# A layer norm inside a scheduled Mamba block: the sum of squares by VectorE or GpSimd and four narrow matmuls, in place of twelve column-group matmuls

## The chip, the cores and the metric

The kernel runs on one core of a Trainium2 chip, as one launch. The metric is the device time of that launch in microseconds (us), as the median of several runs. The profile is one execution of the same program, and its span is counted from the first to the last instruction that the profiler recorded. Engines are named as the profile names them: PE is TensorE's matmuls, PEld its weight loads, DVE is VectorE, ACT is ScalarE, POOL is GpSimd, and SP is SyncE, which issues nearly all DMAs.

## The reference

The input is x of shape (8, 384, 32, 32), taken as eight batches of 1024 tokens with 384 channels. Everything is float32.

```
x = x + mamba(ln_c(x))          # eight batches
t = t + ffn(ln_t(t))            # t = tokens of x; only batches 0 to 4 change

mamba:  t = layernorm(t) * ln_w + ln_b
        xm, z = split(t @ in_proj_w.T)         # 384 -> 2 x 768
        xc = silu(causal_conv3(xm) + conv_b)
        dt, Bm, Cm = split(xc @ x_proj_w.T)    # 24 + 16 + 16
        dt = softplus(dt @ dt_proj_w.T + dt_proj_b)
        h_t = exp(dt*A) * h_(t-1) + dt*xc*Bm ;  y = sum_n h*Cm + xc*D   # 16 states
        t = (y * silu(z)) @ out_proj_w.T
        t = gelu(t @ mlp_w1.T + b1) @ mlp_w2.T + b2
ffn:    two linear layers with sign-binarised weights, each output clipped and
        scaled by the largest absolute value of its batch, a gelu between them
```

Each norm takes a mean and a variance over the 384 channels of a token, subtracts the mean and multiplies by (variance + eps) to the power of -1/2. The reference's norm of x and the first norm of the Mamba block are joined into one in the kernel.

## The kernel before

**Tiles.** Channels lie on the 128 partitions and tokens along the free axis. A batch is cut into two halves of T = 512 tokens, so a normalised tile is [128, 3, 512]: KC = 3 chunks of 128 channels. G = 4, and TG = 128 tokens is a quarter of a half.

**Stages.** For each batch, `s1` does the norm, the input projections (`p_in`, `p_z`), the convolution, the low-rank projection (`p_dbc`, `p_all`, then `p_dt`), and writes its results to DRAM. `s2` does the scan: POOL multiplies, ACT takes the exponential, DVE runs the scan instruction (line 990), and PE adds over the states (`py`, line 929, 1536 matmuls in all, 192 to a batch). `s3` does the output projection and the MLP (`p_out`, `p_h`, `p_o`). `ffn` runs for batches 0 to 4 (`p_y1` and `p_y2`, which the profile shows as p_y).

**The norm.** `norm` (lines 590 to 666) is called 26 times: twice for each of the eight batches in `s1`, and twice for each of five batches in `ffn`. Its steps are, in order: `total` is the sum of the three chunks, by POOL with two adds (lines 628 and 629) or by DVE with one reduction (line 632); a matmul with a 128x128 block of ones gives -C times the mean on every partition (`p_mean`, line 640); DVE subtracts it (line 643); ACT squares the tile into `sq` (line 557). Then `columns` (line 599) sums the squares over the channels: three chunks by four token quarters, twelve matmuls with a [128, 32] block of ones, the quarters lying in four 32-column groups of the array. ACT or DVE scales the sums into SBUF (`var`, line 572 or 579). One matmul with every 32nd column of the identity (`p_turned`, line 654) turns them so that tokens lie on partitions, as [128, 4]. DVE adds eps (line 658), POOL takes the power (line 660), `spread` (line 617) brings the four columns back to a row on all partitions (`p_r`), and DVE multiplies (line 664).

**The order of the work.** Nothing runs in the order in which it is written down. Each step is handed to a planner (`Plan.add`) with an engine, a cost in us, the tiles that it reads and writes, and optionally another engine that may do it (`others`). `Plan.run` then plays the engines forward with those costs, takes the next step for the engine that is free first, and emits the instructions in that order. So a changed step can move any later instruction on any engine. Three more rules of the planner matter here:

- A tile comes from a ring with a fixed number of buffers: `mm` (PSUM) has three, `sq` two, `rstd` two, `root` two, and `dbc` one. A step waits until its ring has a free buffer. In the kernel before, `dbc` is used by the low-rank projection of `s1` alone: from `p_dbc` until `p_dt` has read it and the store `rows_d<-dbc` is done.
- PE pays 0.097 us (`MODE`) in the planner's books whenever it changes between column- or row-tiled matmuls (`tiled=True`) and full ones.
- Where PE would stand idle for over 0.7 us in those books (`IDLE`), the planner emits matmuls whose result nobody reads (`spare`, line 451, 128x256), until the gap is filled. These are real instructions of the program:

```
if e == "PE":
    while now - free[e] > IDLE and self.spare.ring.free[0:] and (...):
        ...
        self.fill()
        free[e] = clock.run(free[e], MM / 2)
```

Every float32 matmul shows up in the trace as two passes: two weight loads and two matmul records.

Of the kernel before, what the change touches and what calls it, by code (L numbers as in the profile page):

```python
# [28 lines left out]
ALU = mybir.AluOpType  # L29
AX = mybir.AxisListType  # L30
# [3 lines left out]
P = 128  # L34
B, C, L = 8, 384, 1024
KC = C // P
# [8 lines left out]
T = 512  # L45
HALVES = [slice(0, T), slice(T, L)]
SQ = 4
DQ = P // SQ
# [4 lines left out]
G = P // DQ  # L53
TG = T // G
# [37 lines left out]
def c_act(n):  # L92
    return 0.2 + n * 0.00084


def c_dve(n):
    return 0.17 + n * 0.00102
# [90 lines left out]
class Plan:  # L188
# [12 lines left out]
    def add(self, engine, cost, emit, r=(), w=(), claim=(), table=None, size=0, others=None,  # L201
            land=1.6, rate=350e3, lag=None, tiled=False):
        op = Op()
        op.engine, op.cost, op.emit, op.table = engine, cost, emit, table
        op.others, op.settle = others or {}, None
        op.size, op.land, op.prio = 0.03 + size / rate, land - 0.1, (*self.prio, len(self.ops))
        op.next, op.ready, op.tiles, op.tiled = [], 0.0, [], tiled
        op.lag = LAG.get(engine, 0.0) if lag is None else lag
        op.slack = SLACK if self.prio[0] < 0 else 0.0
        deps = set()  # L210

        def parts_of(t):
            t, part = t if isinstance(t, tuple) else (t, None)
            if t not in op.tiles:
                op.tiles.append(t)
                if t.ring is not None:
                    t.left += 1
            if part is None:
                if None not in t.parts:
                    t.parts[None] = [None, []]  # L220
                return list(t.parts.values())
            if part not in t.parts:
                whole = t.parts.get(None)
                t.parts[part] = [whole[0], list(whole[1])] if whole else [None, []]
            return [t.parts[part]]

        for t in claim:
            t.left += 1
            op.tiles.append(t)
        for t in r:  # L230
            for p in parts_of(t):
                if p[0] is not None:
                    deps.add(p[0])
                p[1].append(op)
        for t in w:
            for p in parts_of(t):
                if p[0] is not None:
                    deps.add(p[0])
                deps.update(p[1])
                p[0], p[1] = op, []  # L240
        deps.discard(op)
        op.wants = len(deps)
        for d in deps:
            d.next.append(op)
        self.ops.append(op)
        return op
# [144 lines left out]
class Layer:  # L391
# [198 lines left out]
    def norm(self, t, eps, scale):  # L590

        nc, add = self.nc, self.plan.add
        def columns(src, name):
            p = self.piece("mm", [P, TG], name)

            def emit():
                for k in range(KC):
                    for g in range(G):
                        nc.tensor.matmul(
                            p.real[g * DQ : (g + 1) * DQ, :], self.ones[:, :DQ],  # L600
                            src.real[:, k, g * TG : (g + 1) * TG],
                            start=(k == 0), stop=(k == KC - 1),
                        )

            add("PE", 0.79, emit, r=[src], w=[p], tiled=True)
            return p

        def spread(src, name, turned=False):
            p = self.piece("mm", [P, T], name)

            def emit():
                for g in range(G):
                    if turned:
                        by, of = src.real[:, g : g + 1], self.ident
                    else:
                        by, of = self.ident[:, g * DQ : g * DQ + 1], src.real
                    nc.tensor.matmul(
                        p.real[:, g * TG : (g + 1) * TG], by.to_broadcast([P, P]), of,
                        start=True, stop=True,
                    )  # L620

            add("PE", 0.89, emit, r=[src], w=[p])
            return p

        total = self.piece("sq", [P, T], "total")

        def in_two():
            nc.gpsimd.tensor_add(total.real, t.real[:, 0, :], t.real[:, 1, :])
            nc.gpsimd.tensor_add(total.real, total.real, t.real[:, 2, :])

        def at_once():
            nc.vector.tensor_reduce(
                total.real, t.real.rearrange("p k l -> p l k"), AX.X, ALU.add
            )

        add("POOL", 2.5, in_two, r=[t], w=[total], others={
            "DVE": (c_dve(KC * T) + 0.02, at_once)
        })
        p_mean = self.piece("mm", [P, T], "p_mean")
        add("PE", MM, lambda: nc.tensor.matmul(  # L640
            p_mean.real, self.ones, total.real, start=True, stop=True
        ), r=[total], w=[p_mean])
        add("DVE", c_dve(KC * T) + 0.05, lambda: nc.vector.scalar_tensor_tensor(
            t.real, p_mean.real.unsqueeze(1).to_broadcast([P, KC, T]), -1.0 / C, t.real,
            ALU.mult, ALU.add,
        ), r=[p_mean], w=[t])

        sq = self.piece("sq", [P, KC, T], "sq")
        self.act(lambda: sq.real, lambda: t.real, AF.Square, c_act(KC * T), r=[t], w=[sq])
        p_var = columns(sq, "p_var")  # L650
        var = self.piece("rstd", [P, TG], "var")
        self.affine(lambda: var.real, lambda: p_var.real, [p_var], [var], scale=scale, n=TG)
        p_turned = self.piece("mm", [P, G], "p_turned")
        add("PE", 0.14, lambda: nc.tensor.matmul(
            p_turned.real, var.real, self.ident[:, ::DQ], start=True, stop=True
        ), r=[var], w=[p_turned])
        rstd = self.piece("root", [P, G], "rstd")
        add("DVE", 0.15, lambda: nc.vector.tensor_scalar_add(rstd.real, p_turned.real, eps),
            r=[p_turned], w=[rstd])
        add("POOL", 1.0, lambda: nc.gpsimd.tensor_tensor(  # L660
            rstd.real, rstd.real, self.power.to_broadcast([P, G]), ALU.pow
        ), w=[rstd])
        p_r = spread(rstd, "p_r", True)
        add("DVE", c_dve(KC * T), lambda: nc.vector.tensor_mul(  # L664
            t.real, t.real, p_r.real.unsqueeze(1).to_broadcast([P, KC, T])
        ), r=[p_r], w=[t])
# [738 lines left out]
```

## Time and profile before

| | |
|---|---|
| runs | 3205.4, 3207.55, 3211.03 us; median 3207.55 |
| profiled execution | 3206.13 us, span 3204.3 us, so 1.8 us lie around the span |
| granted TensorE clock, mean | 0.987 |
| busy in the span | PE 3087.3, POOL 2803.7, DVE 2602.2, ACT 2021.0 us |
| DMA | 751.78 MB, 235 GB/s over the span |

A group of the profile is written as "line engine operation out<-in, shapes, count, then busy us and mean ns of one, then the idle time of the engine just before these instructions and what ended it". In the chain of waits each piece is what released the next one, followed back from the last instruction. A PE record lasts until the result is out, and records overlap, so the busy time of a group is the better price of a matmul than the mean of one record.

### The profile page before, as it was taken

To read this page: it belongs to the slowest core of one execution; us is meant where nothing else is said; L and a number is where in the kernel's file an instruction comes from. 1 tells how busy PE (TensorE), PEld (TensorE's weight loads), DVE (VectorE), ACT (ScalarE), POOL (GpSimd) and SP (SyncE) were. 2 spreads that over 40 slices of the span, in tenths; PEclk is the share of its full clock that TensorE was granted. 3 is DMA by queue.
4 is the path that set the end of the run, shared out by engine and by line. 5 is a ranking of instruction groups with operands and counts; after the bars stand their busy time and mean duration, and the time that the engine had idled before them with its cause. 6 is when DMAs were issued, how large, how long until landed. Compare 5 with 4: busy or idle time off the path is not lost.

```text
span 3204.3 us, 32487 instructions
## 1 busy us (share of the span) xinstructions
PE 3087.3 (96%) x10286; PEld 1265.2 (39%) x10286; DVE 2602.2 (81%) x2058; ACT 2021.0 (63%) x2397; POOL 2803.7 (87%) x1097
## 2 busy tenths in 40 slices
PE   9898999998999999999999999999999999999999
PEld 4333433343433443444344334343344443333333
DVE  4787887889978789787898888997788977887881
ACT  4878786767666565665675576457566565655662
POOL 2878988989989888999988999999989999998890
PEclk9899999999999999999999999999999999999999
DMA  7888878767777667766687686777768756756542
GB/s 236 293 290 303 272 230 305 267 213 250 241 287 249 202 204 248 261 229 221 207 296 239 212 301 213 253 229 278 239 223 268 235 184 216 232 179 191 162 153 72
DMA packets 348970, 751.78 MB, mean 235 GB/s; under 512 B 36480, under 2 KB 113792, under 8 KB 339584
## 3 DMA queue, kind: packets, MB, share of 16 engines
q1 hardware_dynamic: 348368, 749.61, 70.3%
q8 instruction: 83, 1.36, 0.2%
q14 instruction: 87, 0.71, 0.1%
q10 hardware_dynamic: 432, 0.09, 0.0%
HBM read 569.21 MB, written 180.36 MB: 234 GB/s over the span
## 4 chain that ended last, share of the span: by engine, by line
PE 62%; DVE 12%; DMA 9%; POOL 7%; ACT 6%; issue 3%; SPq 1%; DVEq 0%; POOLq 0%; ACTq 0%
PE p_y L541 15%; PE p_h L541 11%; PE p_o L541 10%; PE py L929 8%; PE p_out L541 6%; POOL u L965 5%; PE p_z L541 5%; PE p_in L541 5%; DVE u L990 4%; DVE da L990 3%; ACT da L557 2%; DMA dtx_r<-dtx_d 2%; ACT L557 2%; DMA dt_r<-dt_d 1%; PE spare L451 1%
## 5 line engine op out<-in xcount | busy, mean ns | idle before, releaser
L557 ACT ACTIVATE da<-dt_r,a_neg 128x1024 f32<-128x1024 f32 (+1 forms) x960 | 898.9, 944 | 596.0 <-DVE u L990 320.4
L965 POOL TENSOR_TENSOR u<-dtx_r,bc 128x2048 f32<-128x2048 f32 (+1 forms) x360 | 1185.5, 3309 | 87.6 <-PE py L929 49.1
L965 POOL TENSOR_TENSOR u<-u,bc 128x2048 f32<-128x2048 f32 (+1 forms) x274 | 900.0, 3291 | 140.9 <-DVE u L990 129.2
L990 DVE TENSOR_TENSOR_SCAN u<-da,u 128x1024 f32<-128x1024 f32 (+1 forms) x436 | 869.9, 2007 | 160.2 <-ACT da L557 80.6
L541 PE MATMUL p_h<-t,w_b 128*128 128x512 f32 x1152 | 515.7, 601 | 16.5 <-DMA w_b<-in_mlp_w 13.8
L541 PE MATMUL p_o<-g,w 128*128 128x512 f32 x1152 | 514.5, 600 | 6.4 <-DMA w<-in_mlp_w 4.7
L990 DVE TENSOR_TENSOR_SCAN da<-da,dtx_r 128x1024 f32<-128x1024 f32 (+1 forms) x192 | 382.0, 2015 | 64.0 <-POOL dtx_r L965 45.0
L965 POOL TENSOR_TENSOR dtx_r<-dtx_r,bc 128x2048 f32<-128x2048 f32 (+1 forms) x120 | 396.6, 3310 | 1.9
L541 PEld LDWEIGHTS p_h<-t,w_b 128*128 128x128 f32 x1152 | 215.0, 191 | 307.7 <-issue 264.0
L541 PEld LDWEIGHTS p_o<-g,w 128*128 128x128 f32 x1152 | 216.3, 191 | 298.0 <-issue 280.2
L541 PE MATMUL p_y<-tn,w_b 128*128 128x512 f32 x720 | 320.1, 600 | 7.7 <-DVE tn L664 3.4
L541 PE MATMUL p_y<-gf,w_n 128*128 128x512 f32 x720 | 321.9, 600 | 5.4 <-ACT dt L572 2.6
L929 PE MATMUL py<-u,fold 128*32 128x512 f32 x2304 | 306.7, 630 | 7.5 <-POOL u L965 7.5
L990 DVE TENSOR_TENSOR_SCAN da<-da,u 128x1024 f32<-128x1024 f32 (+1 forms) x140 | 281.8, 2038 | 34.0 <-ACT da L557 18.4
L557 ACT ACT_TABLE_LOAD x211 | 270.7, 1283 | 6.5 <-DMA dt_r<-dt_d 2.8
L541 PE MATMUL p_out<-yg,w 128*128 128x512 f32 x552 | 244.9, 596 | 3.4 <-ACT dt L572 1.8
L541 PE MATMUL p_in<-t,w_f 128*128 128x512 f32 x504 | 230.2, 605 | 15.5 <-ACT t L572 4.4
L541 PE MATMUL p_z<-t,w_f 128*128 128x512 f32 x504 | 232.4, 609 | 12.3 <-DMA w_f<-in_in_proj_w 7.7
L541 PEld LDWEIGHTS p_y<-tn,w_b 128*128 128x128 f32 x720 | 135.0, 191 | 189.5 <-issue 168.3
L541 PEld LDWEIGHTS p_y<-gf,w_n 128*128 128x128 f32 x720 | 134.6, 191 | 189.3 <-issue 170.9
L572 ACT ACTIVATE y<-p_y,v_vecs 128x512 f32<-128x512 f32 x145 | 98.8, 681 | 130.7 <-PE p_y L541 104.0
L572 ACT ACTIVATE g<-p_h,v_vecs 128x512 f32<-128x512 f32 x159 | 108.0, 679 | 114.1 <-PE p_h L541 113.6
(132 smaller groups left out, 3267.4 us busy)
## 6 DMA issues: line engine op xcount, KB each, us to landing
dtx_r<-dtx_d SPq DMA_DIRECT2D x72, 1024.0 KB, 6.0
dt_r<-dt_d SPq DMA_DIRECT2D x144, 512.0 KB, 5.1
w_b<-in_mlp_w SPq DMA_DIRECT2D x192, 192.0 KB, 3.4
w<-in_mlp_w SPq DMA_DIRECT2D x96, 384.0 KB, 3.3
w_f<-in_in_proj_w SPq DMA_DIRECT2D x168, 192.0 KB, 4.6
y_d<-y SPq DMA_DIRECT2D x120, 256.0 KB, 4.8
gf<-y_d SPq DMA_DIRECT2D x60, 512.0 KB, 6.7
xc_d<-xc SPq DMA_DIRECT2D x48, 512.0 KB, 6.5
```

The source lines that it names most:

```text
L451: self.plan.fill = lambda: self.nc.tensor.matmul(self.plan.spare.real[:, : 2 * P], self.ones, self.one.to_broadcast([P, 2 * P]), start=Tru ...
L541: self.nc.tensor.matmul(p.real, w.real[:, w0 + k, :], t.at(k0 + k), start=start and k == 0, stop=stop and k == n - 1,)
L557: lambda: self.nc.scalar.activation(out(), in_(), func, **{k: v() if callable(v) else v for k, v in kw.items()}),
L572: nc.scalar.activation(out(), in_(), AF.Identity, bias=bias, scale=scale)
L929: nc.tensor.matmul(py.real[g * DQ : (g + 1) * DQ, :], self.fold, hc, start=False, stop=(q == NQUAD - 1), skip_group_check=True,)
L965: nc.gpsimd.tensor_mul(u.real[:, x], t.real[:, x], row.real.unsqueeze(2).to_broadcast([P, n, 2]))
L990: da=da, in_u=in_u: nc.vector.tensor_tensor_scan(to(i), da.real[:, i, :], in_u(i), state.real[:, col : col + 1] if half else 0.0, ALU.mult ...
```

## The change

The twelve matmuls of `columns`, the scaled copy `var` and the matmul that turned it are taken out. The squares of the three chunks are added into a [128, 512] tile `squared`: by DVE with one reduction, or by POOL with two adds where the planner finds POOL free. Four matmuls then take a quarter of `squared` each as weights and a single column of ones as the moving operand, which sums over the channels and turns in one step. The scale moves into the instruction that adds eps. The tile `squared` comes from the ring `dbc`; `var` no longer takes a buffer of the ring `rstd`, and `p_var` none of the ring `mm`. The new matmuls are not marked as tiled, and the planner books them with 0.56 us, where it booked 0.79 for `columns` and 0.14 for the turn.

```diff
     def norm(self, t, eps, scale):
 
         nc, add = self.nc, self.plan.add
-        def columns(src, name):
-            p = self.piece("mm", [P, TG], name)
-
-            def emit():
-                for k in range(KC):
-                    for g in range(G):
-                        nc.tensor.matmul(
-                            p.real[g * DQ : (g + 1) * DQ, :], self.ones[:, :DQ],
-                            src.real[:, k, g * TG : (g + 1) * TG],
-                            start=(k == 0), stop=(k == KC - 1),
-                        )
-
-            add("PE", 0.79, emit, r=[src], w=[p], tiled=True)
-            return p
-
...
         sq = self.piece("sq", [P, KC, T], "sq")
         self.act(lambda: sq.real, lambda: t.real, AF.Square, c_act(KC * T), r=[t], w=[sq])
-        p_var = columns(sq, "p_var")
-        var = self.piece("rstd", [P, TG], "var")
-        self.affine(lambda: var.real, lambda: p_var.real, [p_var], [var], scale=scale, n=TG)
+        squared = self.piece("dbc", [P, T], "squared")
+
+        def two_sums():
+            nc.gpsimd.tensor_add(squared.real, sq.real[:, 0, :], sq.real[:, 1, :])
+            nc.gpsimd.tensor_add(squared.real, squared.real, sq.real[:, 2, :])
+
+        def one_sum():
+            nc.vector.tensor_reduce(
+                squared.real, sq.real.rearrange("p k l -> p l k"), AX.X, ALU.add
+            )
+
+        add("DVE", 1.83, one_sum, r=[sq], w=[squared], others={"POOL": (2.5, two_sums)})
         p_turned = self.piece("mm", [P, G], "p_turned")
-        add("PE", 0.14, lambda: nc.tensor.matmul(
-            p_turned.real, var.real, self.ident[:, ::DQ], start=True, stop=True
-        ), r=[var], w=[p_turned])
+
+        def turn():
+            for g in range(G):
+                nc.tensor.matmul(
+                    p_turned.real[:, g : g + 1], squared.real[:, g * TG : (g + 1) * TG], self.one,
+                    start=True, stop=True,
+                )
+
+        add("PE", 0.56, turn, r=[squared], w=[p_turned])
         rstd = self.piece("root", [P, G], "rstd")
-        add("DVE", 0.15, lambda: nc.vector.tensor_scalar_add(rstd.real, p_turned.real, eps),
-            r=[p_turned], w=[rstd])
+        add("DVE", 0.15, lambda: nc.vector.tensor_scalar(
+            rstd.real, p_turned.real, scale, eps, ALU.mult, ALU.add
+        ), r=[p_turned], w=[rstd])
```

## The prediction

> **What bounds the kernel now.** I read the page's busy times first, then the chain of waits, then the groups with their shapes kept apart, then the timeline where spare matmuls stand. From the page:
>
> ```profile
> PE 3087.3 (96%) x10286; PEld 1265.2 (39%) x10286; DVE 2602.2 (81%) x2058; ACT 2021.0 (63%) x2397; POOL 2803.7 (87%) x1097
> PEclk9899999999999999999999999999999999999999
> PE 62%; DVE 12%; DMA 9%; POOL 7%; ACT 6%; issue 3%; SPq 1%; DVEq 0%; POOLq 0%; ACTq 0%
> ```
>
> PE is busy for all but 117.0 of 3204.3 us, and 62% of the chain is PE work. The clock is full nearly everywhere, so no time is to be won there. PE is one queue in order, so the span is the useful PE work, plus the spare matmuls, plus the idle time that is left. I work with that identity: a change must alter one of the three terms. The spare matmuls are inside the 3087.3, and they are in the chain. The longest pieces of the chain, in order of time, hold three runs of them, 23.84 us together:
>
> ```profile
> 2.98 7.09 PE spare L451 x26
> ...
> 1310.09 10.66 PE spare L451 x48
> ...
> 2601.92 6.09 PE spare L451 x28
> ```
>
> The timeline around the second run shows how a run stands among the norm's steps (start, length, engine, line):
>
> ```profile
> 1306.63 1.51 PE L599 MATMUL p_var<-sq,small 128*32 128x128 f32 x24 [2.73 <-ACT dt L572]
> 1308.07 1.90 PE L451 MATMUL spare<-small 128*128 128x256 f32 x4
> ...
> 1309.81 0.28 PE L654 MATMUL p_turned<-ident,var 128*128 128x4 f32 x2
> 1310.03 10.72 PE L451 MATMUL spare<-small 128*128 128x256 f32 x48
> ...
> 1320.58 5.31 PE L541 MATMUL p_out<-yg,w 128*128 128x512 f32 x12
> ```
>
> The projection after the run starts with no idle time before it: the run occupied PE to its end. A spare pass in a run costs 10.72 / 48 = 0.223 us. The groups that the change touches or that price it, by shape:
>
> ```profile
> L451 PE MATMUL spare<-small 128*128 128x256 f32 x322 | 81.3, 394 | 1.2 <-ACT z L570 0.9 <-DVE rstd L658 0.3
> L617 PE MATMUL p_r<-ident,rstd 128*128 128x128 f32 x208 | 30.5, 295 | 11.1 <-POOL rstd L660 8.1 <-DVE rstd L658 3.0
> L599 PE MATMUL p_var<-sq,small 128*32 128x128 f32 x624 | 23.1, 283 | 10.3 <-ACT sq L557 5.8 <-ACT dt L572 3.5 <-DVE t L664 0.7
> L654 PE MATMUL p_turned<-ident,var 128*128 128x4 f32 x52 | 9.0, 244 | 3.3 <-ACT var L572 1.1 <-DVE var L579 0.8 <-ACT z L570 0.8
> L572 ACT ACTIVATE var<-p_var 128x128 f32<-128x128 f32 x22 | 5.9, 270 | 6.7 <-PE p_var L599 6.5
> L632 DVE TENSOR_REDUCE total<-t 128x512 f32<-128x1536 f32 x2 | 3.8, 1923 | 1.8 <-DMA t<-in_x 1.8
> L629 POOL TENSOR_TENSOR total<-total,t 128x512 f32<-128x512 f32 x14 | 17.8, 1272 | 1.1
> ```
>
> **Useful PE work.** Removed: 23.1 us of p_var and 9.0 us of p_turned, 32.1 us over 26 norms, or 1.23 us for a norm. Added for a norm: four matmuls, so eight passes, each with a 128x128 weight load and one moving column. No row shows that. The nearest is p_r, also eight passes with 128x128 weights for a norm, but with 128 moving columns: 30.5 / 26 = 1.17 us. From above, the old p_turned with four columns: 9.0 / 52 = 0.173 us a pass, 1.38 us a norm. From below, p_var's 23.1 / 624 = 0.037 us a pass, with weights of a quarter of the width, 0.30 us a norm. The three give 30.5, 36.0 and 7.7 us over 26 norms, so useful work moves by -1.6, +3.9 or -24.4 us. I take -2, from p_r: what passes of full weights cost next to each other is mostly not the stream. So the twelve matmuls were cheap because they ran four column groups at once, and little is saved.
>
> The Trainium skill ("TensorE: Matmul & The Clock Gate", section "LDWEIGHTS (loading the stationary operand)") says that a load is timed by its number of columns, P/1.2 ns, and not by what is streamed after it. By that, eight loads of 128 columns would be an estimated 0.85 us for a norm and the term about -10 us; no row of this trace has so narrow a stream of full weights.
>
> **Spare matmuls.** The instruction lists of both built programs hold 161 spare matmuls before (322 passes in the trace) and 293 after, 132 more. All other PE instructions are equal in number, bar the norm's. Counted by the scan's 192 py matmuls for each batch, they go from 50, 7, 1, 32, 0, 1, 60, 9, with 1 behind the last, to 102, 25, 20, 6, 0, 20, 87, 32, with 1 behind the last. 47 of the 132 lie ahead of the first 128 py, where the pipeline fills. The reason can be read from the norm's steps. The chain of one norm was p_var, var, p_turned, and is now a DVE reduction of 1.92 us and a turn. The reduction sits in DVE's queue among the scans, so the projections that need the norm come later. Also, `squared` takes the only `dbc` buffer: in the order of emission it follows a low-rank projection's dbc 14 times, and a dbc follows it 14 times.
>
> Price: 264 passes at the run's 0.223 us are 59 us; at the group's mean of 81.3 / 322 = 0.2525 they are 66.7 us. 237 of the 293 stand in runs of four or more, so I take 59. In the worst case for this step, none of it costs anything, because PE would have stood idle there; that is a rival below.
>
> **DVE, POOL, ACT, SP.** DVE: 24 of 26 sums fall to it, 24 x 1.92 = 46.1 us. It loses 4 var (1.2 us) and 2 total reductions (3.8 us). Copies that ACT and DVE share shift by about -2.9 us (it gives up 12 of some 0.76 us and takes 9 of some 0.70). Sum +38 us, on an engine with 602 us idle. POOL: 2 sums and 2 totals more, each two adds of 1.27 us, +10 us. ACT: 22 var less (-5.9), 8 table loads more in the program (at 1.283 us, +10.3), and some 5.6 us of those shared copies, together +10 us. SP: one more store of a weight piece, and the loads are issued in the new order. What of this makes PE wait is what the planner filled with spare matmuls; I do not count it again. Cover gone, all of DVE's 38 us would be late for a scan.
>
> **Idle time of PE.** p_var and p_turned had 13.6 us of idle time before them, and the new turn will wait for the reduction instead; I take no change. What is queued behind the new waits: a reduction on DVE that waits for its buffer holds up the scans behind it, and PE's py and POOL's second product wait for these. Ten of DVE's reductions (and one sum on POOL) wait for a DMA in the instruction lists, the store of the previous dbc tile or a load beside it:
>
> ```profile
> rows_d<-dbc SPq DMA_DIRECT2D x16, 64.0 KB, 5.9
> ```
>
> That tile's landing takes 1.6 to 8.6 us, 5.9 in the median. An issue-to-landing at the median where 1.6 had been counted on is 4.3 us late, 11 x 4.3 = 47 us if every one is felt. From below it is 0, since the store leaves before the three p_dt pairs that hold the buffer as well. DVE's share of the chain is 12%, so I take 0 and keep half, 24 us, for the upper end.
>
> **Sum.** 3204.3 - 2 + 59 + 0 = 3261.3 us of span. With 1.8 us around the span, 3263.1 us for an execution like the profiled one; the median of the runs before is 1.4 us above that execution, so 3264.5, rounded to 3264 us: 1.8% slower.
>
> **The rivals.**
>
> *The spare matmuls are free.* They would ride in idle time that PE has anyway: the identity then has its third term smaller. Place: the pipeline's start and the spots at 1310 and 2602 us. For it: there are 117 us of idle time, more than 59. Against it: that idle time is scattered in waits of a few us at most on projections (16.5 us before p_h, 15.5 before p_in, 12.3 before p_z), while spare passes come in runs, and the chain runs through these. If all is absorbed the time is 3207.5 - 2 = 3205.5, and with the narrow matmuls midway to their lowest price (-12) 3195 us. It decides from the point where PE's idle time falls from 117 to under 60 us. I give 0.13: 0.08 for faster, 0.05 for no change.
>
> *The single dbc buffer costs on top.* The late stores hold DVE's queue, and the waits are not in the planner's books. Half of the 47 us gives 3288, and all of it 3311. For it: the eleven waits. Against it: p_dt holds the buffer for several us after the store too, so most landings are over by then. 0.17.
>
> *The PE sum*, as worked out: 0.70. That the change does not do what it says can hardly be: POOL takes only two of the sums, but the squares are added as stated.
>
> **How the numbers follow.** The range: from below, half of the 59 us absorbed and -10 us for the narrow matmuls reach 3225. From above, 66.7 for 59 (+8), the dear narrow matmuls (+6) and 24 us of late stores reach 3302. I give 3225 to 3302. A difference under 0.2% (6.4 us) is about what a measurement of this kernel cannot tell from none. Slower: 0.70 + 0.17 = 0.87; same 0.05; faster 0.08.
>
> **What would show it.** Right: PE busy near 3144 us, spare near 586 passes and 131 to 148 us, the new p_turned at 208 passes and near 30 us busy, idle time of PE near 117, reductions of squared 24 times near 1.92 us, DVE near 2640. Wrong in the first rival's way: PE idle time under 70 us. In the second's: DVE idle time before L642 of over 20 us, ended by PE or a DMA, and PE's idle time over 140 us. Wrong in the price: p_turned at 8 us busy.

## The result, and the profile after

The changed kernel takes 3236.01 us (median of 3 runs, 3232.92 to 3236.28) against 3207.55 us. The ratio is 1.0088, with a 95% interval of 1.0069 to 1.0106: slower by 28.5 us, half of the 56.5 us that were forecast, and inside the range. The profiled execution took 3236.28 us with a span of 3234.5 us, so 30.2 us more of span than before. Of all the executions behind the times below, one (3295.9 us at a granted clock of 0.94, in e5) ran in a slower state of the chip and is in no time or ratio that is given.

The page's busy times, clock and chain of the changed kernel:

```profile
PE 3138.7 (97%) x10082; PEld 1319.7 (41%) x10082; DVE 2638.4 (82%) x2073; ACT 2026.8 (63%) x2384; POOL 2815.8 (87%) x1107
PEclk9999999999999999999999999999999999999999
PE 60%; DVE 13%; DMA 9%; ACT 9%; POOL 5%; issue 4%; SPq 1%; DVEq 0%; POOLq 0%; ACTq 0%
```

PE is busy 51.4 us longer (3138.7 - 3087.3) and idle 21.2 us less (95.8 instead of 117.0); together that is the span's 30.2 us. The groups of the changed kernel, by shape (out<-in, count, busy us, mean ns, then idle time before and what ended it):

```profile
L451 PE MATMUL spare<-small 128*128 128x256 f32 x586 | 156.1, 412 | 1.0 <-DVE xc L737 0.8
L602 PE MATMUL p_r<-ident,rstd 128*128 128x128 f32 x208 | 30.9, 296 | 3.1 <-POOL rstd L661 1.5 <-ACT dt L572 1.5
L651 PE MATMUL p_turned<-small,squared 128*128 128x1 f32 x208 | 29.9, 265 | 17.9 <-DVE squared L642 13.5 <-DVE rstd L658 2.9 <-ACT dt L557 1.4
L642 DVE TENSOR_REDUCE squared<-sq 128x512 f32<-128x1536 f32 x24 | 45.8, 1907 | 12.4 <-PE p_dt L802 8.1 <-ACT sq L557 3.1 <-PE p_turned L651 1.1
L541 PE MATMUL p_z<-t,w_f 128*128 128x512 f32 x504 | 224.5, 596 | 2.4 <-issue 2.4
L930 PE MATMUL py<-u,fold 128*32 128x512 f32 x2304 | 300.4, 621 | 0.0
```

The same two useful groups before:

```profile
L541 PE MATMUL p_z<-t,w_f 128*128 128x512 f32 x504 | 232.4, 609 | 12.3 <-DMA w_f<-in_in_proj_w 7.7 <-DVE tn L643 1.6 <-ACT z L570 1.4
L929 PE MATMUL py<-u,fold 128*32 128x512 f32 x2304 | 306.7, 630 | 7.5 <-POOL u L965 7.5
```

The identity of the prediction closes: spare matmuls +74.8 us (156.1 - 81.3), the norm's matmuls -2.2 (29.9 for 32.1), and the rest of PE's work 51.4 - 74.8 + 2.2 = -21.2 us. That last term was not in the prediction. The unchanged matmuls became cheaper: p_z by 7.9 us, py<-u by 6.3, with a mean of 596 ns for 609 and 621 for 630. The longest p_z pass of 128x512 took 1192 ns before and 697 ns after. The trace also records when TensorE ran at half its clock: 84.2 us before and 75.5 us after. Laid over the matmul records, 67.4 us of it fell on useful matmuls before and 42.2 us after, and 2.6 and 22.5 us on spare ones. A pass takes about twice its time there (p_z: 1192 ns for a median of 593), so half of such time is lost, and an estimated 12.6 of the 21.2 us come from this. So the added spare matmuls stand partly where PE had been idle, and partly where a half-clock stretch would have been. Whether they cost anything at all is the first question of the experiments.

### The profile page after: what moved, and what is told of

Same layout as the page of the kernel before. It is cut to its first block, busy times and chain, and to the rows that moved or that the text cites. A ratio compares the mean times of both kernels' runs of the same rounds, so it can differ in the third digit from the quotient of the medians.

```text
span 3234.5 us, 32138 instructions
## 1 busy us (share of the span) xinstructions
PE 3138.7 (97%) x10082; PEld 1319.7 (41%) x10082; DVE 2638.4 (82%) x2073; ACT 2026.8 (63%) x2384; POOL 2815.8 (87%) x1107
## 4 chain that ended last, share of the span: by engine, by line
PE 60%; DVE 13%; DMA 9%; ACT 9%; POOL 5%; issue 4%; SPq 1%; DVEq 0%; POOLq 0%; ACTq 0%
PE p_o L541 12%; PE p_y L541 12%; PE p_h L541 9%; PE py L930 7%; PE p_z L541 6%; PE p_in L541 6%; DVE u L991 5%; PE p_out L541 4%; POOL u L966 4%; DVE da L991 3%; ACT da L557 3%; ACT L557 2%; DMA w_b<-in_mlp_w 2%; PE spare L451 2%; DMA dtx_r<-dtx_d 1%
## 5 line engine op out<-in xcount | busy, mean ns | idle before, releaser
L966 POOL TENSOR_TENSOR u<-dtx_r,bc 128x2048 f32<-128x2048 f32 (+1 forms) x360 | 1185.9, 3312 | 81.3 <-PE py L930 45.3
L991 DVE TENSOR_TENSOR_SCAN da<-da,dtx_r 128x1024 f32<-128x1024 f32 (+1 forms) x192 | 381.7, 2017 | 92.8 <-POOL dtx_r L966 75.4
L541 PE MATMUL p_z<-t,w_f 128*128 128x512 f32 x504 | 224.5, 596 | 2.4 <-issue 2.4
```

Source lines behind the costliest of these rows:

```text
L541: self.nc.tensor.matmul(p.real, w.real[:, w0 + k, :], t.at(k0 + k), start=start and k == 0, stop=stop and k == n - 1,)
L966: nc.gpsimd.tensor_mul(u.real[:, x], t.real[:, x], row.real.unsqueeze(2).to_broadcast([P, n, 2]))
L991: da=da, in_u=in_u: nc.vector.tensor_tensor_scan(to(i), da.real[:, i, :], in_u(i), state.real[:, col : col + 1] if half else 0.0, ALU.mult ...
```

## The experiments

The theories: **S**, the spare matmuls delay the work behind them. **G**, they only fill gaps that are there anyway. **C**, they also hold the clock. **B**, the single dbc buffer carries the loss. **O**, the work of the new operations does, above all DVE's sums. **P**, one planned order is simply better than another. Every ratio is to the kernel before on the same chip, whose median was 3201.8 us for e1 to e4, 3202.25 for e5 to e8 and 3204.5 for e9 to e12. The ratios are the estimates on record, with their 95% intervals; they differ by up to 0.1% from the quotient of two medians. In e1, e2, e9 and e10 every engine's instructions stand in the same order as in the kernel they start from, apart from those left out, put in or replaced; in all others the planner made a new order.

**e1 and e2: the same order without the spare matmuls.**

```diff
-        self.plan.fill = lambda: self.nc.tensor.matmul(...)
+        def fill():
+            self.fills += 1
+            if self.fills <= 13:
+                self.nc.tensor.matmul(...)
+        self.plan.fill = fill
```

> The changed kernel with the same planned order on every engine, but only the first 13 of its 293 spare matmuls are issued; the other 280 are left out. They cost 280 x 2 x 0.266 us = 149 us of busy PE in the profile after. Theory S, the spare matmuls delay the work behind them: PE busy falls by some 149 us and the time by 30 us or more, to 3206 or below. Theory G, they stand in gaps that are there anyway: the time stays within 10 us of 3236, and PE's idle time grows from 96 to over 220 us. Theory C, they also hold the clock: more half-clock stretches fall on useful matmuls, p_z, p_in and py get dearer by over 20 us together, and the time is longer than 3236.

> The kernel before with the same planned order, only the first 13 of its 161 spare matmuls issued; 148 left out, 148 x 2 x 0.2525 = 75 us of busy PE. It says whether the changed kernel is slower without any spare matmul too. Theory S: the time falls by 15 us or more below 3207, and the difference to e1 is under 10 us. Theory G: 3207 within 10 us, and the difference to e1 stays near 28 us: then the order of the useful work, not the spare matmuls, carries the loss. Theory C: slower than 3207.

Measured: e1 3251.95 us, ratio 1.0151 (1.0124 to 1.0179). e2 3210.19 us, ratio 1.0022 (1.0010 to 1.0035). The busy times, e1 first, then e2:

```profile
PE 3066.7 (95%) x9522; PEld 1231.9 (38%) x9522; DVE 2637.9 (81%) x2073; ACT 2026.7 (63%) x2384; POOL 2814.8 (87%) x1107
```

```profile
PE 3057.1 (95%) x9990; PEld 1220.9 (38%) x9990; DVE 2604.1 (81%) x2058; ACT 2020.4 (63%) x2397; POOL 2803.9 (87%) x1097
```

And their granted clocks, e1 first, then e2:

```profile
core 0: 3239.2 us, clock 0.969
```

```profile
core 0: 3213.6 us, clock 0.974
```

In e1 148.6 us of spare matmuls are gone, yet PE's busy time falls by 72.0 us only and its idle time rises from 95.8 to 172.5. The other 76.6 us went into useful matmuls that ran slower: the trace shows 200.6 us at half clock where the changed kernel has 75.5, and a mean granted clock of 0.969 for 0.988. In e2 the half-clock time goes from 84.2 to 170.5 us.

The second run of spare matmuls that the prediction showed, at 1310 us, is gone in e2 (start, length, engine, line):

```profile
1315.68 0.59 PE L661 MATMUL p_turned<-ident,var 128*128 128x4 f32 x2 [1.52 <-ACT var L579]
...
1316.13 6.33 PE L548 MATMUL p_out<-yg,w 128*128 128x512 f32 x8
...
1326.39 3.78 PE L548 MATMUL p_out<-yg,w 128*128 128x512 f32 x4 [3.93 <-DMA yg<-yg_d]
```

The first eight passes of p_out do start at once, where the run had held them back by over 10 us. But they run at a mean granted clock of 0.58, where the kernel before had 1.00; the last four wait 3.93 us for a DMA and run at 0.50. From the start of p_turned to the end of the twelfth pass it is 14.49 us in e2 and 16.08 in the kernel before: of 10.7 us of spare matmuls 1.6 are won.

S falls as a net cost: nothing gets faster without spare matmuls. That they delay some work, and that most of what is won without them is lost again to the clock and to other waits, is what this one spot shows; e1 and e2 show the balance alone. e2 fits G and C. In e1 G's sign, over 220 us of idle time, was not reached; e1 fits C: its p_in, py and p_z groups with 128x512 streams from w_f, u and dtx_r grew by 29 us together (10.6, 15.7 and 2.8), and its time is above 3236. The changed kernel is still slower than the one before with neither having more than 13 of them: 1.0151 / 1.0022 = 1.013. So the loss does not lie in the spare matmuls; it lies in the order and the work that are left, and in part perhaps in the clock, since e1 has 30 us more at half clock than e2.

**e3: a buffer of its own for squared.**

```diff
-            "rstd": ring("rstd", 2), "root": ring("root", 2),
+            "sqd": ring("sqd", 1), "root": ring("root", 2),
...
-        squared = self.piece("dbc", [P, T], "squared")
+        squared = self.piece("sqd", [P, T], "squared")
...
-        dynamic_dma_scratch_size=1024
+        dynamic_dma_scratch_size=512
```

> The changed kernel with a buffer of its own for squared in place of the one dbc buffer (the ring rstd, which has no user any more, and half of the DMA scratch space make room). The plan then has 202 spare matmuls where it had 293, and 20 DVE sums where it had 24. Theory B, the single dbc buffer carries the loss: DVE's idle time before the sums that PE's p_dt ends (8.1 us) goes, and the time falls by 20 us or more, to 3216 or below. Theory O, the reduction on DVE and the later norm carry it: 3230 to 3240. By the sum over PE, 91 spare matmuls less at the rate seen (132 more cost 30 us of span) give -21 us, 3215.

Measured: 3235.6 us, ratio 1.0101 (1.0081 to 1.0121). The sums on DVE, by shape:

```profile
L642 DVE TENSOR_REDUCE squared<-sq 128x512 f32<-128x1536 f32 x20 | 38.1, 1903 | 1.7 <-ACT sq L557 1.7
```

The wait for p_dt (8.1 us in the changed kernel) is gone, and so are 91 spare matmuls. The time is no better than the changed kernel's 1.0088, so nothing speaks for B. But e3 is also another order (and gives POOL 6 of the sums, where it had 2), and e5 to e8 show that an order alone can move the time by up to 1%; a gain that this hid is not excluded. The number of spare matmuls was no gauge of the time here.

**e4: the sum over the chunks alone, with the old turn.** The sum is written as in the change, and `columns` then takes four matmuls, one for each token quarter.

```diff
+        squared = self.piece("dbc", [P, T], "squared")
...
-        p_var = columns(sq, "p_var")
+        p_var = columns(squared, "p_var")
```

> One part of the change alone: squares added over the chunks by DVE or POOL into the dbc buffer, as in the changed kernel, but summed over the channels by four column-group matmuls, scaled into var and turned as before. 216 spare matmuls in the plan. Theory O or B (the sum or its buffer carries the loss, the narrow matmuls nothing): 3225 to 3245. If the narrow matmuls carry it: 3207 to 3215. By the count of spare matmuls alone, 55 more than before at 30 / 132 us each: 3220.

Measured: 3223.34 us, ratio 1.0073 (1.0051 to 1.0095). A loss of most of the size is there without the narrow matmuls. Since e4 is another order too, this does not show how much of it is the sum's.

**e5 to e8: other orders of the same operations.** Only the planner's number for the power, a step that both kernels share, is changed: to 0.97 in e5 and e6, as below, and in the same line to 1.05 in e7 and e8. e5 and e7 start from the kernel before, e6 and e8 from the changed one.

```diff
-        add("POOL", 1.0, lambda: nc.gpsimd.tensor_tensor(
+        add("POOL", 0.97, lambda: nc.gpsimd.tensor_tensor(
             rstd.real, rstd.real, self.power.to_broadcast([P, G]), ALU.pow
         ), w=[rstd])
```

> The kernel before, every instruction of the norm as it was; only the number that the planner books for POOL's power (a step that both kernels share) is 0.97 us instead of 1.0. That gives another order with 178 spare matmuls instead of 161. Theory P, the loss of the changed kernel is one order happening to be worse than another: this moves by 10 us or more from 3202, up or down. Theory O, the loss belongs to the operations: this stays within 8 us of the kernel before.

> The changed kernel with the same edit, 0.97 us booked for POOL's power; 258 spare matmuls instead of 293. Theory O: within 8 us of the changed kernel, at a ratio of 1.006 to 1.011 to the kernel before. Theory P: it moves by 10 us or more, and the difference to its pair e5 is not near 28 us.

> The kernel before with 1.05 us booked for POOL's power, a third order, 178 spare matmuls. Theory P: 10 us or more away from the kernel before, most likely slower, since the order of the kernel before has the fewest spare matmuls of the three. Theory O: within 8 us of it.

> The changed kernel with 1.05 us booked for POOL's power, 253 spare matmuls. Theory O: ratio 1.006 to 1.011 to the kernel before, and 28 us, give or take 8, above its pair e7. Theory P: somewhere from 3200 to 3250, not tied to e7.

Measured: e5 3232.42 us, ratio 1.0100 (1.0076 to 1.0123). e6 3226.8 us, 1.0083 (1.0062 to 1.0104). e7 3214.1 us, 1.0046 (1.0026 to 1.0065). e8 3240.5 us, 1.0118 (1.0094 to 1.0142). With no step of the norm changed, the kernel before loses up to 1.0%, as much as the whole change. An order here includes which engine takes a step that several may do: in e7 DVE does 6 of the 26 totals, where it did 3. In e5's profile the 30.4 us of added span are 14.6 us of idle time of PE, 8.0 of spare matmuls and 7.8 of other matmuls:

```profile
PE 3103.1 (96%) x10320; PEld 1276.8 (39%) x10320; DVE 2603.7 (80%) x2062; ACT 2035.3 (63%) x2410; POOL 2801.7 (87%) x1094
```

e6 is even a little faster than its pair e5. P holds in part: an order is worth as much as the effect that is to be explained. O is not excluded, since the changed kernel's orders are all between 1.0083 and 1.0118.

**e9: the changed kernel's order with a smaller sum.** It leaves the squares of two chunks out.

```diff
         def one_sum():
-            nc.vector.tensor_reduce(
-                squared.real, sq.real.rearrange("p k l -> p l k"), AX.X, ALU.add
-            )
+            nc.vector.tensor_copy(squared.real, sq.real[:, 0, :])
```

> The changed kernel with its instructions, order and waits as they are on all five queues, but DVE's 24 sums are a plain copy of the first chunk; the squares of the other two chunks are left out of the variance there. That takes some 24 x 1.3 us = 30 us of DVE's work away under the same order. Theory O, the work of the sums is what is paid: the time falls by 15 to 30 us, to a ratio of 1.004 or below. Theory P, the order is what is paid: it stays within 6 us of the changed kernel, at 1.007 to 1.011.

Measured: 3252.01 us, ratio 1.0143 (1.0125 to 1.0162), slower than the changed kernel. The groups of e9 show that the edit did not take DVE's work away:

```profile
L642 DVE COPY squared<-sq 128x512 f32<-128x512 f32 x24 | 49.4, 2058 | 11.5 <-PE p_dt L800 7.2 <-ACT sq L557 3.3 <-PE p_turned L649 1.1
```

A copy of 512 elements took 2058 ns in the mean, longer than the reduction of 1536 (1907). It ranged from 410 to 4519 ns. The timeline of e9 shows why (start, length, engine):

```profile
2473.70 4.08 POOL L964 TENSOR_TENSOR u<-u,bc 128x2048 f32<-128x2048 f32 x1
...
2474.24 3.82 DVE L642 COPY squared<-sq 128x512 f32<-128x512 f32 x1 [1.55 <-ACT sq L557]
...
2477.74 4.26 POOL L964 TENSOR_TENSOR dtx_r<-dtx_r,bc 128x2048 f32<-128x2048 f32 x1
```

The copy ends at 2478.06, 0.28 us after the end of the POOL product that was running (2477.78). In the trace 20 of the 24 copies end like this, 0.28 to 0.33 us after the end of a product of POOL. The four that met none took 410 to 428 ns. The nine products of 128x2048 that POOL began next, before the copy was over, took 4.09 to 4.28 us, where 4.09 is the mean. The reductions of the changed kernel show none of this: 1885 to 1958 ns in all 24. The Trainium skill ("GPSIMD Engine Reference", section "1. Specifications") says that POOL's SBUF interfaces are shared with VectorE, with contention where a DVE instruction runs in a two-port mode or has two SBUF inputs; the ends of these copies agree, though no row shows in which mode a copy ran. So the edit exchanged one load for another, and e9 decides nothing between O and P.

**e10: the kernel before, same order, with DVE's work added.**

```diff
             def emit():
+                nc.vector.tensor_reduce(self.unused, src.real, AX.X, ALU.add)
                 for k in range(KC):
                     for g in range(G):
```

> The kernel before, order and waits the same on all five queues, with one instruction more for each norm: DVE adds the squares along the tokens into three columns that nobody reads, 26 reductions of 1536 elements, some 26 x 1.6 us = 42 us of DVE's work. Theory O: slower by 15 us or more (ratio over 1.005). Theory P: DVE has 602 us of idle time, so at most 8 us slower.

Measured: 3219.38 us, ratio 1.0047 (1.0032 to 1.0063), 15 us. The busy times and the added group:

```profile
PE 3091.1 (96%) x10286; PEld 1266.8 (39%) x10286; DVE 2643.5 (82%) x2084; ACT 2020.1 (63%) x2397; POOL 2803.8 (87%) x1097
```

```profile
L598 DVE TENSOR_REDUCE unused<-sq 128x3 f32<-128x1536 f32 x26 | 45.2, 1738 | 2.3 <-ACT sq L558 2.3
```

Between the two expectations: 45.2 us of DVE's work, whose result nobody waits for, cost 15 us although DVE has some 600 us of idle time. That is a third of its length, with every queue's order kept. PE's idle time shows most of it: 126.4 us for 117.0. The extra reader of sq also keeps that buffer a little longer. The trace has one wait for it, 1.6 us of ACT, so little of the 15 us is seen to come that way; no run tells the two apart.

**e11: no sum over the chunks at all.** The tile squared and both ways of the sum are taken out as well.

```diff
             for g in range(G):
-                nc.tensor.matmul(
-                    p_turned.real[:, g : g + 1], squared.real[:, g * TG : (g + 1) * TG], self.one,
-                    start=True, stop=True,
-                )
+                for k in range(KC):
+                    nc.tensor.matmul(
+                        p_turned.real[:, g : g + 1], sq.real[:, k, g * TG : (g + 1) * TG],
+                        self.one, start=(k == 0), stop=(k == KC - 1),
+                    )
-        add("PE", 0.56, turn, r=[squared], w=[p_turned])
+        add("PE", 2.8, turn, r=[sq], w=[p_turned])
```

> No sum over the chunks on DVE or POOL and no squared tile: twelve narrow matmuls, 24 passes, sum and turn straight from sq. 192 spare matmuls in the plan. By the trace after, 8 narrow passes are 29.9 / 26 = 1.15 us busy, so 24 are about 3.4 us and PE gets 26 x 2.3 = 60 us of work more than in the changed kernel. By the sum over PE: 60 us more, less 101 spare matmuls at 0.53 us, so near the changed kernel, 3225 to 3250 us. If a DVE hop in the norm is what costs: near or under the kernel before.

Measured: 3251.3 us, ratio 1.0155 (1.0136 to 1.0174). The busy times of e11 and the group of its narrow matmuls:

```profile
PE 3173.3 (98%) x10296; PEld 1341.1 (41%) x10296; DVE 2607.8 (80%) x2062; ACT 2015.1 (62%) x2373; POOL 2801.9 (86%) x1094
```

```profile
L641 PE MATMUL p_turned<-small,sq 128*128 128x1 f32 x624 | 81.7, 264 | 5.6 <-ACT sq L557 5.5
```

The 24 narrow passes of a norm are 81.7 / 26 = 3.14 us of PE, 0.131 us each. PE's idle time falls to 75.4 us, and the time lies just above what the sum over PE had given. Without the hop to DVE this version was not faster. Against the kernel before, PE has 49.6 us more of the norm's matmuls, 19.9 more of spare ones, 16.5 more in all others, and 41.6 less of idle time. Against the changed kernel the 51.8 us of added narrow matmuls are balanced by 54.9 us less of spare ones; what grew is the other matmuls, by 37.7 us. The clock goes with that: 150.4 us at half clock for 75.5, of which 122.0 fell on useful matmuls for 42.2.

```profile
core 0: 3248.7 us, clock 0.977
```

So the expected range was nearly met, but not by the sum that gave it, and this one order does not tell the price of the hop from that of the order.

**e12: a fourth order of the kernel before.**

```diff
-            add("PE", 0.79, emit, r=[src], w=[p], tiled=True)
+            add("PE", 0.83, emit, r=[src], w=[p], tiled=True)
```

> The kernel before with 0.83 us booked for the twelve column-group matmuls instead of 0.79: a fourth order of the same operations, with 135 spare matmuls, the fewest of all. If the number of spare matmuls tells how good an order is: 3185 to 3200, faster than the kernel before. If it tells nothing: anywhere from 3200 to 3235, as the other two orders.

Measured: 3213.3 us, ratio 1.0027 (1.0012 to 1.0042). The order with the fewest spare matmuls (135) is not the fastest. e5 and e7 both have 178 and lie at 1.0100 and 1.0046. Among these orders the number does not tell the time. No version that was run beats the kernel before.

## Why the prediction came out as it did

**The direction was right, and the path to it was not.** The forecast put the whole loss into the spare matmuls: +59 us, with the idle time taken as unchanged. They measured +74.8 us of busy time, but e1 and e2 show that they cost nothing net, because without them the time grows by 0.2% and by some 0.6%. PE's idle time fell by 21.2 us and its other matmuls by another 21.2 us, and these are what the forecast left out of the identity. The step that failed is the reading of "The projection after the run starts with no idle time before it: the run occupied PE to its end" as a cost. The run did hold p_out back, but in e2, without it, only 1.6 of its 10.7 us were won: p_out ran at a lower clock and then waited for a DMA. That a run of spare matmuls lies on the chain does not show that the work behind it could have ended earlier. Of the clock, "so no time is to be won there" failed with it: half-clock time on useful matmuls went from 67.4 to 42.2 us. That the time came out inside the range is therefore luck as far as the cause goes: a loss of another kind, 28.5 us, fell to the lower part of a range that was made for spare matmuls.

**The first rival had the mechanism of the spare matmuls, but not the consequence.** They do ride in gaps and on half-clock stretches. The kernel is still slower, and in e1, with the same order and all but 13 of them gone, it stays slower; so something other than the spare matmuls makes it longer. PE's idle time, 95.8 us, met neither that rival's sign (under 70) nor the forecast's (near 117).

**Useful PE work: right.** p_turned was forecast at 30.5 us from p_r and took 29.9. By the figure of the Trainium skill ("TensorE: Matmul & The Clock Gate", section "LDWEIGHTS (loading the stationary operand)") it would have been an estimated 22 us. The eight passes cost nearly what p_r's eight passes cost (30.9 us), so the stream's width was not, for the most part, what they are paid for.

**DVE: the work was right and its price was not.** 24 reductions at 1907 ns and DVE at 2638.4 us agree with the forecast of 1.92 us and 2640. But "What of this makes PE wait is what the planner filled with spare matmuls; I do not count it again" left it at nothing beside them: e10, with as many spare matmuls as the kernel before, prices 45.2 us of it at 15 us. For +38 us that would be an estimated 13 us of the 28, if these sums cost at the same rate; no run shows that they do.

**The dbc buffer: right to be left small.** The waits were there, 8.1 us before five sums, all ended by PE's p_dt; none that the trace shows was ended by the late store. e3 removed them without a gain, in another order.

**The rest is, by argument, the order.** The operations of the kernel before were measured in four orders: 1, 1.0027, 1.0046, 1.0100. Those of the change were measured in three: 1.0083, 1.0088, 1.0118. The means are 1.0043 and 1.0096, 0.53% or 17 us apart, near what e10 gives for DVE's work. The kernel before is the best of its four orders and lies 14 us below their mean; the changed kernel lies 3 us below its own. 17 + 14 - 3 gives the 28 us. That is an argument from seven orders with overlapping ranges; how the 28.5 us divide is not shown more closely than that, and the cause stays open to that extent. A run of the new operations in the very order of the kernel before was not tried.

## What to carry to other kernels

Where a planner or scheduler sets the order, a change of one step is also a change of order, and here the order alone moved the time by up to 1.0%; measure two or three perturbed orders of both kernels before a difference of that size is put down to the change. Filler work on an engine's chain is not shown to cost anything until a run without it is faster: count what idle time and which slow stretches it stands in. An engine with 600 us of idle time still charged, in e10, a third of the 45 us of work that was added to it, so "off the bottleneck" is worth a price of its own and not zero.

## What the runs showed of the hardware

- With all but 13 spare matmuls gone, the time at half TensorE clock went from 84.2 to 170.5 us (order of the kernel before) and from 75.5 to 200.6 us (order of the change), while the time rose by 0.2% and, from 1.0088 to 1.0151, by 0.6%. So the filler matmuls, the clock that they held and what they delayed taken together, were worth 0.2 to 0.6% of the time here, although the half-clock time without them more than doubled.
- A float32 copy of 128x512 on DVE from SBUF to SBUF took 410 to 428 ns in the four cases that met no product of POOL; the other 20 ended only 0.28 to 0.33 us after one, and took up to 4519 ns (e9). A reduction of three times as many elements kept its 1.9 us.
- A matmul pass with 128x128 float32 weights and a single moving column cost 0.131 us (e11) to 0.144 us (29.9 / 208), nearly as much as one with 128 columns (30.9 / 208 = 0.149).
